# A hand-ordered cross-attention kernel: a new order of all engines and transfers up to the first attention sum of the end stage, banks picked one by one, and row-by-row exponentials in four words

## The chip, the cores and the metric

The kernel runs on one core of a Trainium2 chip, as one program. The metric is device time in microseconds, here the median of three runs. A profile is one execution of the same program, taken by the hardware profiler; its span is the time from the first to the last instruction.

## What is computed

Two batches of 2048 tokens (640 channels) attend with 20 heads of 32 channels to two sets of 77 keys: text, and image prompts with weights of their own. All data are float32.

```python
q = split_heads(x @ Wq.T)
k, v = split_heads(text @ Wk.T), split_heads(text @ Wv.T)
out_text = merge_heads(softmax(q @ k.T / sqrt(32)) @ v)
k_ip, v_ip = split_heads(ip @ Wk_ip.T), split_heads(ip @ Wv_ip.T)
out_ip = merge_heads(softmax(q @ k_ip.T / sqrt(32)) @ v_ip)
return (out_text + out_ip) @ Wo.T + bo + x
```

## The kernel before

All matrices come with the contracted dimension first. The channels lie in 5 chunks of 128, which are 4 heads (g = 0 to 3) each. Ten pairs q = (batch, chunk) are worked through, each as two units of 1024 tokens, u = 2q and 2q + 1. A unit has two halves h of 512 tokens, or 8 blocks of 128 tokens, and these go in three groups s of 3, 3 and 2 blocks. A group is 4 heads x n blocks x 2 key sets of 77, so 24 or 16 rows of 77 scores for each token.

PSUM has eight banks of 512 numbers (`banks`, named bank_67 to bank_74 in the program). A group of scores fills four, one for each head; before the change these are always the first or the last four (`halves`).

The order of the whole kernel is written out by hand, as a list of words (`SCHEDULE`). The loop at the end emits them one after the other; each engine does its own in that order, and waits only for data, or for a place that is still read. The words:

- q.u.h: queries of unit u and half h, five matmuls of 128 x 512 (L206); cq copies them out of their bank, scaled, on ScalarE (L220).
- k.c.y and v.c.y: keys and values of chunk c and key set y (L144); ck and cv copy them (ScalarE); SQ.c turns the values in squares of 32 (VectorE, L154); VS.q.half spreads them over the partitions with 8 small transfers (SP, L160).
- Rs.u: scores of group s (L242). Ks.u: their four copies, one a bank, to SBUF (ScalarE, L254). M: row maxima (VectorE, L290). S: subtraction (GpSimd, L304). E: exponential of the group (ScalarE, L310). D: row sums (VectorE, L315), I: their reciprocals (L320), N: the product with them (GpSimd, L325), T: a transposition in squares of 32 (VectorE, L332).
- A.q: attention sum of a pair (L341), which needs all six T of its two units and both spreads; CA copies it (L364, L368).
- o, p, m: products with Wo for the two batches (L480, L499, L509); co and cm add them to x and bo on VectorE; G and W are sums on GpSimd that these products use.
- LK, LQ, LX, LO load weights of keys and values, weights of queries, tokens, and Wo. SF and SS fetch a part of x to `acc` and store a result. All these are issued by SP, strictly in order.

Three sets name groups that go other ways. In BIASED the subtraction falls away: each row's exponential takes its maximum as a bias, with one instruction a row (`exponential_of`, L278). In DIRECT the maxima (L293) and these exponentials also read the scores from PSUM, so K falls away and the banks stay taken until the exponentials have read them. In SUMMED the exponential sums its row too (a second instruction a row), so D falls away.

From 19 us to 427 us TensorE goes through these words up to A.9, the attention sum of the last pair. Then 66 products of a fast matrix scheme (L887) end the kernel.

Of the kernel before, what the change touches and what calls it, by code (L numbers as in the profile page):

```python
# [9 lines left out]
F32 = mybir.dt.float32  # L10
# [10 lines left out]
def kernel(  # L21
# [25 lines left out]
    nc = tc.nc  # L47
# [3 lines left out]
    G = P // D  # L51
# [13 lines left out]
        (11, 0), (12, 0), (13, 0), (13, 2), (14, 0), (14, 2), (15, 1), (15, 2), (18, 1), (19, 2),  # L65
    }
    BIASED = {
        (2, 2), (3, 2), (4, 2), (6, 2), (8, 2), (9, 2), (11, 2), (12, 1), (16, 2), (17, 2), (18, 2),
    }
    SUMMED = {  # L70
        (4, 2), (11, 2), (12, 0), (13, 0), (13, 2), (14, 0), (15, 1), (15, 2), (16, 2), (17, 2), (18, 1),
        (18, 2), (19, 2),
# [13 lines left out]
    halves = banks[:G], banks[G:]  # L86
# [145 lines left out]
    def rows_of(u, s):  # L232
        return keys_of(u, s).rearrange("p n g (t l) -> p (n g) t l", l=L)
# [36 lines left out]
    def exponential_of(u, s, ps=None, den=None):  # L270

        n = GROUPS[s][1]
        for g in range(G):
            for t in range(n):
                for x in range(2):
                    row = rows_of(u, s)[:, t * G + g, x]
                    one = t * G + g, slice(x, x + 1)
                    nc.scalar.activation(  # L278
                        row,
                        row if ps is None else rows_in(ps[g], n)[:, t, x],  # L280
                        AF.Exp,
                        bias=maxs[(u, s)][:, *one],
                        accum_out=None if den is None else den[:, *one],
                    )
# [300 lines left out]
    for t in range(2):  # L585

        ps = halves[t][G - 2 + t]
        project_kv(t, ps)
        for b in range(B):
            nc.scalar.copy(kT[:, 0, b, t, :], keys_in(ps)[:, b])  # L590
# [73 lines left out]
    def emit(word):  # L664
        name, _, where = word.partition("@")
        k, *args = name.split(".")
        x, y = (*(int(a) for a in args if a.isdigit()), None, None)[:2]
        i = int(k[1:]) if k[1:].isdigit() else None
        if k[0] == "R":
            at[name] = halves[int(where)]  # L670
            scores(x, i, at[name])
        elif k == "A":
            at[name] = halves[int(where)]
# [262 lines left out]
```

## Time and profile before

| | |
|---|---|
| device time, median of 3 runs (lowest to highest) | 495.86 us (495.68 to 496.0) |
| the profiled execution: span | 494.6 us |
| transfers | 69.38 MB in 67105 packets, mean 140 GB/s |
| costliest line of TensorE, L206 | 34% of the chain that ended last |
| costliest line of GpSimd, L325 | 176.0 us in 60 instructions |
| costliest line of VectorE, L332 | 115.9 us in 60 instructions |
| costliest line of ScalarE, L254 | 85.3 us in 200 instructions |

A row of the chain or of a timeline gives start, length, engine, line, and how many instructions were merged. An engine's row gives busy time and mean duration, then its idle time before the group and what ended that. SPq is SP's issue of transfers: its length is issue time only, and the landing comes later. Each matmul in float32 shows twice, so a query word is x10 and a group of 12 score matmuls x24.

### The profile page before, as it was taken

What the parts mean: (1) busy time and instruction counts of PE and PEld (TensorE: products, weight loads), DVE (VectorE), ACT (ScalarE), POOL (GpSimd) and SP (SyncE); (2) the same over time, 40 slices, a digit from 0 to 9 for tenths busy, and PEclk for the clock granted to TensorE, in tenths of its full rate; (3) what the DMA queues carried; (4) which work ended last, traced back from release to release, by engine and by line L of the source; (5) the groups of instructions that cost most, each with busy time, mean ns of one, the idle gap of its engine ahead of it and who ended that gap; (6) DMA issues with size and microseconds to landing.
All of it is one profiled execution on the core that took longest, in us unless ns stands there. A gap on an engine that the chain in (4) does not pass through costs nothing.

```text
span 494.6 us, 10484 instructions
## 1 busy us (share of the span) xinstructions
PE 489.1 (99%) x4116; PEld 287.7 (58%) x4116; DVE 413.9 (84%) x416; ACT 309.5 (63%) x1002; POOL 370.5 (75%) x158
## 2 busy tenths in 40 slices
PE   9999999999999999999999999999999999999997
PEld 5666648558557556456566654754755675444443
DVE  0069989989899989979988896687789898999996
ACT  1275788977687778677899786587889862100000
POOL 0069988988988988879886758475689899798700
PEclk9999999999999999999999999999999999999999
DMA  8992046203241724895540666455550212320125
GB/s 278 350 288 80 17 124 181 67 1 95 62 150 44 247 65 146 270 345 178 161 172 27 215 195 223 134 172 183 184 169 19 90 42 85 129 85 2 42 85 212
DMA packets 67105, 69.38 MB, mean 140 GB/s; under 512 B 5488, under 2 KB 47088, under 8 KB 67056
## 3 DMA queue, kind: packets, MB, share of 16 engines
q1 hardware_dynamic: 66048, 67.54, 43.7%
q10 hardware_dynamic: 1008, 1.18, 0.7%
q8 instruction: 32, 0.52, 0.4%
q14 instruction: 17, 0.14, 0.1%
HBM read 54.94 MB, written 10.49 MB: 132 GB/s over the span
## 4 chain that ended last, share of the span: by engine, by line
PE 96%; DMA 3%; ACTq 0%; ACT 0%; DVE 0%; DVEq 0%; issue 0%
PE bank L206 34%; PE bank L887 12%; PE bank L341 11%; PE bank L242 11%; PE bank L499 10%; PE bank L144 9%; PE bank L480 7%; PE bank L509 3%; DMA aT<-in_L_xattn_Wk_ip_dram 2%; DMA x<-in_x_dram 1%; ACTq L538 0%; ACT pb L254 0%; ACTq L552 0%; DVE acc L830 0%; DVEq L931 0%
## 5 line engine op out<-in xcount | busy, mean ns | idle before, releaser
L325 POOL TENSOR_TENSOR pb<-pb,rden 128x1848 f32<-128x1848 f32 (+1 forms) x60 | 176.0, 2943 | 30.4 <-DVE rden L320 23.6
L304 POOL TENSOR_TENSOR pb<-pb,mx 128x1848 f32<-128x1848 f32 (+1 forms) x39 | 121.6, 3129 | 55.4 <-DVE mx L290 55.3
L206 PE MATMUL bank<-x,wq 128*128 128x512 f32 x280 | 125.4, 598 | 0.1
L332 DVE STREAM_TRANSPOSE pb<-pb 128x1920 f32<-128x1920 f32 (+1 forms) x60 | 115.9, 1938 | 9.1 <-POOL pb L325 8.9
L290 DVE TENSOR_REDUCE mx<-pb 128x24 f32<-128x1848 f32 (+1 forms) x50 | 91.6, 1844 | 32.1 <-ACT pb L254 31.9
L254 ACT COPY pb<-bank 128x462 f32<-128x462 f32 (+1 forms) x200 | 85.3, 542 | 29.3 <-PE bank L242 28.9
L315 DVE TENSOR_REDUCE den<-pb 128x24 f32<-128x1848 f32 (+1 forms) x47 | 88.9, 1895 | 15.6 <-ACT pb L310 12.8
L206 PEld LDWEIGHTS bank<-x,wq 128*128 128x128 f32 x280 | 51.7, 190 | 60.0 <-issue 58.8
L310 ACT ACTIVATE pb<-pb 128x1848 f32<-128x1848 f32 (+1 forms) x39 | 65.6, 1684 | 17.5 <-POOL pb L304 17.4
L278 ACT ACTIVATE pb<-bank,mx 128x77 f32<-128x77 f32 x208 | 60.4, 387 | 6.5 <-DVE mx L293 6.5
L278 ACT ACTIVATE pb<-pb,mx 128x77 f32<-128x77 f32 x184 | 54.1, 356 | 1.9 <-DVE mx L290 1.8
L341 PE MATMUL bank<-pb,v 32*32 32x512 f32 x1600 | 55.2, 597 | 0.0
L206 PE MATMUL bank<-x,aT 128*128 128x512 f32 x116 | 51.8, 596 | 0.0
L242 PEld LDWEIGHTS bank<-kT,qT 32*128 32x128 f32 x1024 | 36.1, 184 | 21.6 <-issue 13.3
L144 PE MATMUL bank<-wo_ct,aT 128*128 128x154 f32 x320 | 46.0, 297 | 0.7 <-DMA aT<-in_L_xattn_Wk_ip_dram 0.4
L144 PEld LDWEIGHTS bank<-wo_ct,aT 128*128 128x128 f32 x320 | 43.0, 188 | 4.7 <-issue 3.0
L242 PE MATMUL bank<-kT,qT 32*128 32x154 f32 x1024 | 45.1, 305 | 0.0
L278 ACT ACTIVATION_READ_ACCUMULATOR pb<-bank,mx 128x1 f32 x168 | 44.0, 266 | 0.0
L341 PEld LDWEIGHTS bank<-pb,v 32*32 32x32 f32 x1600 | 29.0, 103 | 22.7 <-issue 10.1
L480 PE MATMUL bank<-aT,wo_ct 128*128 128x512 f32 x80 | 36.3, 595 | 0.0
L206 PEld LDWEIGHTS bank<-x,aT 128*128 128x128 f32 x116 | 21.4, 190 | 23.7 <-issue 23.5
L220 ACT ACTIVATE qT<-bank 128x512 f32<-128x512 f32 x32 | 19.3, 631 | 23.4 <-PE bank L206 23.4
(83 smaller groups left out, 524.2 us busy)
## 6 DMA issues: line engine op xcount, KB each, us to landing
x<-in_x_dram SPq DMA_DIRECT2D x20, 1280.0 KB, 6.7
out_dram<-acc SPq DMA_DIRECT2D x19, 256.0 KB, 2.9
x<-in_x_dram SPq DMA_DIRECT2D x17, 256.0 KB, 5.9
acc<-in_x_dram SPq DMA_DIRECT2D x16, 256.0 KB, 4.4
out_dram<-x SPq DMA_DIRECT2D x15, 256.0 KB, 2.0
v<-vS SPq DMA_DIRECT2D x160, 20.0 KB, 2.7
aT<-in_L_xattn_Wk_dram SPq DMA_DIRECT2D x5, 512.0 KB, 6.0
aT<-in_L_xattn_Wk_ip_dram SPq DMA_DIRECT2D x5, 512.0 KB, 5.5
```

Source lines behind the costliest of these rows:

```text
L144: nc.tensor.matmul(keys_in(out), loaded[n][:, k, :], cT[:, k, :, t, :], start=(k == 0), stop=(k == NCC - 1))
L206: nc.tensor.matmul(pq, weight_of(q)[:, k, :], xs[place_of(u, h)][:, k, :], start=(k == 0), stop=(k == NC - 1), skip_group_check=loose,)
L242: nc.tensor.matmul(ps[g][:, ts(t, 2 * L)], qTs[(u, h)][g * D : (g + 1) * D, ts(st, P)], kT[g * D : (g + 1) * D, c, b].rearrange("p t l -> ...
L254: nc.scalar.copy(keys_of(u, s)[:, :, g], ps[g][:, : n * 2 * L].rearrange("p (n l) -> p n l", n=n))
L278: nc.scalar.activation(row, row if ps is None else rows_in(ps[g], n)[:, t, x], AF.Exp, bias=maxs[(u, s)][:, *one], accum_out=None if den i ...
L290: nc.vector.tensor_reduce(mx, rows_of(u, s), AX.X, ALU.max, negate=negate)
L304: nc.gpsimd.tensor_tensor(rows_of(u, s), rows_of(u, s), maxs[(u, s)].unsqueeze(3).to_broadcast([P, n, 2, L]), ALU.subtract)
L315: nc.vector.tensor_reduce(den_of(u, s), rows_of(u, s), AX.X, ALU.add)
L325: nc.gpsimd.tensor_tensor(rows_of(u, s), rows_of(u, s), rdens[(u, s)].unsqueeze(3).to_broadcast([P, n, 2, L]), ALU.mult)
L332: nc.vector.transpose(p, p)
L341: nc.tensor.matmul(pa[r][g * D : (g + 1) * D, :], v4s[q % 2][rows, g, k, :], zones[rows, :, g, k, :], start=(k == 0), stop=(k == NK - 1),)
L480: nc.tensor.matmul(ps, wo[:, k, ts(NC - 1, P)], rows_of_attention(b, k)[:, i], start=(k == 0), stop=(k == NC - 1),)
```

## The change

Four things change. The order of words up to m4.3 and A.9 is a new one, while the words themselves stay nearly all the same; behind A.9 the order is as before, and only the numbers of banks differ. A group of scores or an attention sum no longer takes a half of the banks: its word lists four banks, in the order in which the heads take them. The exponential of a group is now four words, Es.u.0 to Es.u.3, one a head, so that other work of ScalarE can go between them; for a group that is neither DIRECT nor BIASED the first word does it all, and the others do nothing. And the three sets are drawn anew: DIRECT shrinks from ten groups to five, BIASED grows from 11 to 15, SUMMED has 13 as before.

```diff
     DIRECT = {
-        (11, 0), (12, 0), (13, 0), (13, 2), (14, 0), (14, 2), (15, 1), (15, 2), (18, 1), (19, 2),
+        (11, 0), (13, 0), (15, 1), (18, 1), (19, 2),
     }
     BIASED = {
-        (2, 2), (3, 2), (4, 2), (6, 2), (8, 2), (9, 2), (11, 2), (12, 1), (16, 2), (17, 2), (18, 2),
+        (0, 2), (2, 2), (4, 2), (5, 2), (6, 2), (9, 2), (11, 2), (12, 0), (12, 1), (13, 2), (15, 2), (16, 2),
+        (17, 2), (18, 2), (19, 1),
     }
     SUMMED = {
-        (4, 2), (11, 2), (12, 0), (13, 0), (13, 2), (14, 0), (15, 1), (15, 2), (16, 2), (17, 2), (18, 1),
-        (18, 2), (19, 2),
+        (0, 2), (2, 2), (4, 2), (5, 2), (6, 2), (11, 2), (12, 1), (15, 1), (15, 2), (17, 2), (18, 1), (18, 2),
+        (19, 2),
     }
...
-    halves = banks[:G], banks[G:]
...
-    def exponential_of(u, s, ps=None, den=None):
+    def exponential_of(u, s, g, ps=None, den=None):
         n = GROUPS[s][1]
-        for g in range(G):
-            for t in range(n):
-                for x in range(2):
+        for t in range(n):
+            for x in range(2):
...
-        "q.0.1@5 R0.0@0 cq.0.1 R1.0@1 K0.0 SF.0.0 q.1.0@0 K1.0 M0.0 LK.4 LQ.5 LK.5 M1.0 S0.0 R2.0@1 v.0.0@1 K2.0 "
+        "q.0.1@2 R0.0@6457 cq.0.1 R1.0@0132 K0.0 M0.0 K1.0 q.1.0@6 R2.0@0132 v.0.0@7 S0.0 cq.1.0 v.0.1@6 M1.0 "
...
         if k[0] == "R":
-            at[name] = halves[int(where)]
+            at[name] = [banks[int(n)] for n in where]
             scores(x, i, at[name])
...
                 elif direct or biased:
-                    exponential_of(
-                        x, i, ps if direct else None, den_of(x, i) if (x, i) in SUMMED else None
-                    )
-                else:
+                    if (x, i) in SUMMED and (x, i) not in dens:
+                        den_of(x, i)
+                    exponential_of(x, i, int(args[1]), ps if direct else None, dens.get((x, i)))
+                elif args[1] == "0":
                     exponential(x, i)
```

Three places show how the instructions move. The first is TensorE behind A.4. Before, the last rows of A.4 are followed by q.12.1 and then by the scores R0.11, in the last four banks:

```order
507 L341 MATMUL bank_73<-pb,v_0_80 32x512 x4
508 L341 MATMUL bank_74<-pb,v_0_80 32x512 x4
509 L206 MATMUL bank_68<-x_84,wq_75 128x512 x5
510 L242 MATMUL bank_71<-kT,qT_0_1766 128x154
511 L242 MATMUL bank_72<-kT,qT_0_1766 128x154
512 L242 MATMUL bank_73<-kT,qT_0_1766 128x154
513 L242 MATMUL bank_74<-kT,qT_0_1766 128x154
```

Now R0.11 follows at once, in four banks from both halves:

```order
507 L340 MATMUL bank_73<-pb,v_0_80 32x512 x4
508 L340 MATMUL bank_67<-pb,v_0_80 32x512 x4
509 L242 MATMUL bank_71<-kT,qT_0_1743 128x154
510 L242 MATMUL bank_69<-kT,qT_0_1743 128x154
511 L242 MATMUL bank_70<-kT,qT_0_1743 128x154
512 L242 MATMUL bank_68<-kT,qT_0_1743 128x154
```

The query word q.12.1 has moved behind R0.11, so that scores follow the attention sum directly.

The second place is ScalarE at the same point: the copies of A.4 (L364, L363 after the change) and the direct group E0.11, which reads its four banks (`mx_0` are its maxima). Before:

```order
232 L364 COPY aT<-bank_74 128x16x32
233 L310 ACTIVATE pb<-pb 128x8x154
234 L220 ACTIVATE qT_1_1957<-bank_68 128x512
235 L310 ACTIVATE pb<-pb 128x12x154
236 L278 ACTIVATE pb<-bank_71,mx_0_1968 128x77 x6
237 L278 ACTIVATE pb<-bank_72,mx_0_1968 128x77 x6
238 L278 ACTIVATE pb<-bank_73,mx_0_1968 128x77 x6
239 L278 ACTIVATE pb<-bank_74,mx_0_1968 128x77 x6
```

Now:

```order
242 L363 COPY aT<-bank_67 128x16x32
243 L277 ACTIVATE pb<-bank_71,mx_0_1927 128x77 x6
244 L277 ACTIVATE pb<-bank_69,mx_0_1927 128x77 x6
245 L277 ACTIVATE pb<-bank_70,mx_0_1927 128x77 x6
246 L309 ACTIVATE pb<-pb 128x12x154
247 L277 ACTIVATE pb<-bank_68,mx_0_1927 128x77 x6
```

The group moved ahead of other exponentials and of cq.12.1, and the exponential of another group stands between its third and fourth word. The word R1.11 takes bank_71 and bank_69, and o.0 takes bank_70.

The third place is SP around 190 to 205 us of the profile: spreads (L160), tokens (L188), weights of queries (L194) and Wo (L166). Before:

```order
52 L160 DMA v_0_80<-vS_0_93 32x160 x8
53 L468 DMA res<-in_x_dram 128x512
54 L188 DMA x_83<-in_x_dram 128x5x512
55 L194 DMA wq_75<-in_L_xattn_Wq_dram 128x5x128
56 L160 DMA v_0_80<-vS_0_93 32x160 x8
57 L188 DMA x_84<-in_x_dram 128x5x512
58 L166 DMA wo_ct<-in_L_xattn_Wo_dram 128x5x640
```

Now:

```order
50 L160 DMA v_0_80<-vS_0_93 32x160 x8
51 L194 DMA wq_75<-in_L_xattn_Wq_dram 128x5x128
52 L188 DMA x_83<-in_x_dram 128x5x512
53 L160 DMA v_0_80<-vS_0_93 32x160 x8
54 L166 DMA wo_ct<-in_L_xattn_Wo_dram 128x5x640
55 L188 DMA x_84<-in_x_dram 128x5x512
56 L160 DMA v_1_81<-vS_95 32x160 x8
```

The load of x_83 (LX.12.0, for q.12.0) now stands behind the weights LQ.6, and the load of x_84 (LX.12.1, for q.12.1) behind that of Wo.

More of the change, by code (lines that the diff above doesn't have):

```diff
@@ L268, in den_of @@
         return dens[(u, s)]
-    def exponential_of(u, s, ps=None, den=None):
+    def exponential_of(u, s, g, ps=None, den=None):
         n = GROUPS[s][1]
-        for g in range(G):
-            for t in range(n):
-                for x in range(2):
[L276 to L283, printed above, removed]
-                    )
+        for t in range(n):
+            for x in range(2):
+                row = rows_of(u, s)[:, t * G + g, x]
+                one = t * G + g, slice(x, x + 1)
+                nc.scalar.activation(
+                    row,
+                    row if ps is None else rows_in(ps[g], n)[:, t, x],
+                    AF.Exp,
+                    bias=maxs[(u, s)][:, *one],
+                    accum_out=None if den is None else den[:, *one],
+                )
     def maxima(u, s, ps=None, negate=False):
@@ L585 @@
     for t in range(2):
-        ps = halves[t][G - 2 + t]
+        ps = banks[G * t + G - 2 + t]
         project_kv(t, ps)
@@ L669, in emit @@
         if k[0] == "R":
-            at[name] = halves[int(where)]
+            at[name] = [banks[int(n)] for n in where]
             scores(x, i, at[name])
         elif k == "A":
-            at[name] = halves[int(where)]
+            at[name] = [banks[int(n)] for n in where]
             attend(x, at[name])
@@ L701, in emit @@
                 elif direct or biased:
-                    exponential_of(
-                        x, i, ps if direct else None, den_of(x, i) if (x, i) in SUMMED else None
-                    )
-                else:
+                    if (x, i) in SUMMED and (x, i) not in dens:
+                        den_of(x, i)
+                    exponential_of(x, i, int(args[1]), ps if direct else None, dens.get((x, i)))
+                elif args[1] == "0":
                     exponential(x, i)
```

142 rows, old and new, of the table SCHEDULE are left out of this document.

## The prediction

> **What bounds the kernel now.** I read the page first: busy shares, granted clock, chain.
>
> ```profile
> span 494.6 us, 10484 instructions
> PE 489.1 (99%) x4116; PEld 287.7 (58%) x4116; DVE 413.9 (84%) x416; ACT 309.5 (63%) x1002; POOL 370.5 (75%) x158
> PEclk9999999999999999999999999999999999999999
> PE 96%; DMA 3%; ACTq 0%; ACT 0%; DVE 0%; DVEq 0%; issue 0%
> ```
>
> TensorE is busy for 489.1 of 494.6 us and makes up 96% of the chain that ended last; its clock is granted in full throughout. So the span is the sum of TensorE's own work plus its waits. Next, the list of waits, for TensorE alone:
>
> ```profile
> PE bank L573 <- DVE pb L571: 1.1, 1, 1.1
> PE bank L144 <- DMA aT<-in_L_xattn_Wk_ip_dram: 0.4, 1, 0.4
> PE bank L144 <- DMA wo_ct<-in_ctx_dram: 0.3, 1, 0.3
> ```
>
> All three lie before 19 us, in code that the change leaves as it is. What remains must be looked for inside the busy time, in the chain of waits in order of time (start, length, what):
>
> ```profile
> 19.37 4.29 PE bank L206 x10
> 25.45 4.49 PE bank L206 x10
> 29.94 0.74 PE bank L242 x16
> 91.96 1.74 PE bank L242 x38
> 116.65 1.52 PE bank L242 x40
> 129.06 1.74 PE bank L242 x38
> 166.16 1.75 PE bank L242 x40
> 203.34 1.03 PE bank L242 x24
> 204.38 0.53 ACT pb L254
> 228.53 1.67 PE bank L242 x39
> 230.23 1.10 PE bank L499 x4
> 273.35 1.76 PE bank L242 x40
> 287.55 1.06 PE bank L499 x4
> ```
>
> Two things are to be seen. First, a query word (L206 x10) takes 4.29 us after other full-array work and 4.49 us after scores: 0.20 us for leaving the small tiles. Scores (L242) take 0.74 and 1.52 us for 16 and 40 matmuls, so 0.0325 us each and 0.22 us once per stretch. Second, 40 scores (or 38 recorded of 40) take 1.74, 1.74, 1.75 and 1.76 us at 92, 129, 166 and 273 us in place of 1.52. At 203 us the stretch and its wait for a copy last 1.6 us in place of 1.52, and at 228 us 39 scores with the next product last 2.8 us in place of 2.58. These are short waits for a copy that must empty a bank, 0.1 to 0.24 us each: **about 1.3 us** in all. No wait in the stretch up to the last attention sum is for a DMA.
>
> The Trainium skill (Perfetto Trace Analysis, Identifying the Most-Contended Engine) says that matmul busy time is no good measure for TensorE, and that the busy share of weight loads is one. By that rule the 58% of the row PEld would leave room. The repeated rows above speak against room that an order could use; the rule is the last of the rivals.
>
> **The change, part by part.** The diff adds and removes no matmul. TensorE's words are the same 232, in another order. I counted by the two schedules up to A.9. Full-array words right behind scores or attention: 49 before (45 behind scores, 4 behind attention), 46 after (44 and 2). Stretches of scores: 46 before, 45 after. So 3 x 0.20 + 1 x 0.22 = **-0.8 us**. This is on the path, since nothing covers TensorE's own time.
>
> The other engines get about the same load. Five groups leave DIRECT and need a copy again (two of 12 blocks, three of 8: 2 x 4 x 0.59 + 3 x 4 x 0.44 = 10 us of ScalarE). Groups with exponentials row by row go from 21 to 20, so GpSimd has one subtraction more, 3.3 us. SUMMED stays at 13 groups, with two more small ones and two fewer large ones, which is under 2 us of VectorE. How much room they have, one row of busy times by stretch tells, from the start of A.1 to that of A.2; the row above it is the copy's:
>
> ```profile
> L254 ACT COPY pb<-bank 128x462 f32<-128x462 f32 x136 | 64.7, 590 | 16.6 <-PE bank L242 16.6
> ...
> core 0: us, PE busy (x) PEld busy (x) DVE busy (x) ACT busy (x) POOL busy (x), PEclk, DMA share, GB/s
> 105.72:142.82 37.10, 37.10 (x394) 23.73 (x393) 33.57 (x25) 26.35 (x60) 33.03 (x11) 1.00 0.37 102
> ```
>
> VectorE and GpSimd fill 90% of such a stretch. So 10 us more of ScalarE over ten stretches are covered by TensorE, and cost nothing as long as no copy comes late. What can cost is order: where a word of TensorE stands right behind the thing it needs. I walked the places of the new order where that distance is shortest, each from a fixed point of TensorE.
>
> *Copies.* K words now free banks one by one, and a group of scores takes a bank just freed as its last of four. R0.4, R0.8 and R0.10 still take a bank of a query word that ended only 16 scores (0.63 us) earlier; R0.6 no longer does. In before the three of this kind (R0.4, R0.6, R0.8) cost 0.22 us each; the bank now comes fourth, some 0.1 us later. The word o.1 stands behind a direct group as in before (0.24 us). I take 0.2 us for each: **+0.8 us**; bounds 0.3 and 0.9.
>
> *The direct group E0.11.* The rows of before:
>
> ```profile
> 221.94 2.20 DVE L293 TENSOR_REDUCE mx<-bank 128x6 f32<-128x462 f32 x4
> 222.62 5.27 ACT L278 ACTIVATE pb<-bank,mx 128x77 f32<-128x77 f32 x24
> ```
>
> From the end of A.4: R0.11 takes 1.0 us, its maxima 0.1 + 2.2, then three of its four parts 3 x 1.3 + 0.1; the third bank is free after 7.3 us. TensorE reaches o.0, which writes that bank, after R0.11, q.12.1 and R1.11, 1.0 + 4.49 + 1.0 = 6.5 us. **+0.75 us**, of which R1.11 takes the first 0.3. In before the 5.27 us lay beside o.0, in a bank of the other half. The bounds are 0, if TensorE is late here anyway, and 1.2, if the maxima start late.
>
> *Transfers around q.12.0 and q.12.1.* SP issues in order. The rows of before (the first is the landing time of the 20 loads of 1.28 MB at L188):
>
> ```profile
> DMA to landing us min/median/max: 6.1/6.7/13.6
> 119.50 4.95 SPq L160 DMA_DIRECT2D v<-vS  x8
> 189.48 5.98 SPq L160 DMA_DIRECT2D v<-vS  x8
> 196.18 0.38 SPq L188 DMA_DIRECT2D x<-in_x_dram  x1
> 197.17 7.21 SPq L160 DMA_DIRECT2D v<-vS  x8
> 204.48 0.53 SPq L188 DMA_DIRECT2D x<-in_x_dram  x1
> 205.05 0.52 SPq L166 DMA_DIRECT2D wo_ct<-in_L_xattn_Wo_dram  x1
> 205.68 0.47 SPq L188 DMA_DIRECT2D x<-in_x_dram  x1
> L254 ACT COPY pb<-bank 128x308 f32<-128x308 f32 x64 | 22.1, 440 | 12.7 <-PE bank L242 12.4
> L290 DVE TENSOR_REDUCE mx<-pb 128x16 f32<-128x1232 f32 x16 | 22.5, 1409 | 2.8 <-ACT pb L254 2.6
> ```
>
> In the new order SQ.4 stands behind M2.9, and VS.4.0 waits for SQ.4. From the start of R2.9: copies K2.9 begin after 0.8 us and take 1.4, M2.9 1.4, the first square 0.35, VS.4.0 4.95 to 5.98, LQ.6 0.55; then LX.12.0 lands 6.1 to 6.7 us after its issue. That is 15.6 to 17.2 us. TensorE reaches q.12.0 after R2.9, R1.9, three query words and R2.10 with R0.10, 16.1 us. So 0 to 1.1 us; I take **+0.2 us**, since SP is quiet before VS.4.0 and the 4.95 row is the nearest. Then LX.12.0 0.5, VS.4.1 5 to 7.2 behind these loads, the load of Wo 0.55 and only now LX.12.1, which in before went ahead of Wo. It is issued 15.5 to 18.7 us after R2.9 began. In before the load that took 13.6 us had one of 1.28 MB and Wo ahead of it; with Wo alone I put it between that and 6.7, at about 10. With VS.4.0 at 4.95 and VS.4.1 at 7.21 it lands at 27.7 us, and q.12.1 stands at 28.05. **0 us**; bounds 0 and 4.2 (18.7 + 13.6 - 28.05).
>
> *LK.14 behind VS.2.0.* The word v.3.0 stands 11 us earlier than in before, and its weights are loaded behind a spread.
>
> ```profile
> aT<-in_L_xattn_Wv_dram SPq DMA_DIRECT2D x5, 512.0 KB, 5.5
> ```
>
> From the start of v.2.1: the word and its copy last 2.8 us, M0.5 and I2.4 keep VectorE until about 3.3, then the first square 0.35, VS.2.0 4.95, and 5.5 us to landing: 14.1 us. TensorE gets to v.3.0 after v.2.1, three score words, three others and R2.6, 15.3 us. **0 us**; bounds 0 and 1.0 (a spread of 5.98).
>
> *Ends of chains before A.n.* VectorE's main rows:
>
> ```profile
> L332 DVE STREAM_TRANSPOSE pb<-pb 128x1920 f32<-128x1920 f32 x40 | 86.4, 2161 | 5.5 <-POOL pb L325 5.5
> L315 DVE TENSOR_REDUCE den<-pb 128x24 f32<-128x1848 f32 x35 | 72.0, 2058 | 11.7 <-ACT pb L310 10.5 <-ACT pb L278 1.0
> L290 DVE TENSOR_REDUCE mx<-pb 128x24 f32<-128x1848 f32 x34 | 69.5, 2049 | 29.4 <-ACT pb L254 29.3
> ```
>
> Behind K1.17 and up to A.8 VectorE has 21 words: five maxima and sums and three transposes of these kinds, and thirteen shorter ones, 26.5 us when the 0.08 us by which neighbours overlap is taken off. It starts them 3.75 us after R1.17 began: 30.3 us. TensorE takes 30.3. A.5 and A.6 come out as close. I take +0.1 us each for A.5, A.6 and A.8, **+0.3 us**; bounds 0 and 1.5. Before A.9 the group (19,1) now goes row by row:
>
> ```profile
> 254.75 6.10 ACT L278 ACTIVATE pb<-pb,mx 128x77 f32<-128x77 f32 x24
> ```
>
> From the end of A.8 E1.19 starts when K0.19 is done (6.7 us), takes 6.1, and a quarter of E2.19 1.3 (5.27 / 4): 14.1 us. p.0, which needs that bank, stands at 14.4. **0 us**; bounds 0 and 0.5. The Trainium skill (ScalarE: Activation LUTs, Rules for kernel authors) budgets about 0.3 us per ACTIVATE plus 0.83 ns per element, so 0.36 for a row of 77 and 8.7 for 24: by it p.0 would wait 2.4 us, and the sum would be 2.4 us higher. The measured row says 6.1.
>
> Sum: -0.8 for the switches, -1.3 for the old short waits, +0.8 +0.75 +0.2 +0.3 for the new: **-0.05, taken as -0.25 us** because a wait at one place shortens the next (q.12.0's and E0.11's lie 6 us apart). The profiled execution's span is 494.6 us; the median of the runs, 495.86, lies 1.26 us above it, which I leave. Forecast **495.6 us**.
>
> **Rivals.** A measurement of this kernel can tell about 0.2%, or 1.0 us, from no change: from 494.87 to 496.85 counts as the same.
>
> *The new waits don't come.* If each place has the half microsecond of slack that my rows leave uncertain, only some 0.4 us of waits remain: -0.8 - 1.3 + 0.4 = -1.7, so 494.2 us. For it: the list of waits of before shows none for VectorE or a DMA in this part. Against: E0.11's 0.75 us come from two plain rows. This is also the most that the change can bring, 0.4%: with no wait at all it is -2.1.
>
> *The load behind Wo is late.* If LX.12.1 needs the 13.6 us of the one load that ran behind Wo in before, q.12.1 waits 1.0 to 4.2 us; less the 0.75 that it takes off E0.11, and on top of -0.25, this gives 0 to +3.2, so about 497.4 us. It decides from a landing time of some 11 us on. For it: the only measured load behind Wo. Against: that one had 1.28 MB more ahead.
>
> *The change takes off as much as it adds* is the forecast itself.
>
> *TensorE has room after all.* If its words could follow each other closer, VectorE's 33.57 us would set a stretch of 37.1, and nine of them would save some 32 us: 464 us. The rows of TensorE repeat to 0.01 us whatever stands beside them, so I give it 1%. The Trainium skill's rule on the share of weight loads, above, would allow it.
>
> **How the numbers follow.** Forecast 0.47, waits gone 0.29, late load and like slips (slower) 0.23, TensorE's room 0.01. Faster by over 0.2%: 0.30; within: 0.47; slower: 0.23. The range runs from all new waits gone (494.2, less 0.3 for what the old ones may add up to beyond 1.3) to the upper part of the late load (495.6 + 2.2): 493.9 to 497.8.
>
> **What would show it.** In the changed profile: TensorE's first 19 us equal; query words still 4.29 or 4.49; stretches of 40 scores at 92 and 166 us still near 1.7; a wait of o.0 (L479 there) or R1.11 on ScalarE near 221 us; q.12.1 at or right behind its load. The forecast is wrong if a DMA heads TensorE's list of waits with over 1.5 us, or if VectorE ends a wait before A.5, A.6 or A.8 by over 1 us.

## The result: 503.94 us, 1.5% slower

| | before | after |
|---|---|---|
| device time, median (lowest to highest) | 495.86 us (495.68 to 496.13), 5 runs | 503.94 us (500.81 to 505.76), 5 runs |
| ratio, with its 95% interval | 1 | 1.0154 (1.0127 to 1.018) |
| span of the profiled execution | 494.6 us | 499.0 us |

The forecast was 495.6 us, with a range up to 497.8. The profiled execution of the changed kernel is its shortest run, 500.81 us. So two things are to be explained: 4.4 us that the profile shows, and up to 5 us more that the other runs have, while before its runs agreed within 0.5 us. One run among the experiments below took 2835.2 us, each matmul of 128 x 512 lasting 3.0 us at a granted clock given as 1.0; nothing in its profile says why.

The page of the changed kernel (busy times; granted clock in 40 slices; the queue by which instructions come; shares of the chain that ended last):

```profile
span 499.0 us, 10417 instructions
...
PE 489.8 (98%) x4116; PEld 289.1 (58%) x4116; DVE 417.6 (84%) x401; ACT 314.4 (63%) x991; POOL 371.8 (74%) x159
...
PEclk9999999999999999999999999999999999999999
...
q8 instruction: 32, 0.52, 0.5%
...
PE 71%; DVE 13%; ACT 7%; POOL 3%; DMA 3%; issue 2%; ACTq 0%; DVEq 0%; POOLq 0%
```

TensorE's own work is the same. The chain, which was TensorE's for 96%, now goes through VectorE and ScalarE. TensorE's waits (what for, us in total, times, longest):

```profile
PE bank L498 <- DVE acc L529: 2.4, 1, 2.4
PE bank L572 <- DVE pb L570: 1.1, 1, 1.1
PE bank L498 <- DVE acc L523: 0.8, 1, 0.8
PE bank L242 <- issue: 0.8, 1, 0.8
```

The 1.1 us at the start were there before. New are 2.4 and 0.8 us for VectorE, and 0.8 us in which TensorE waited for nothing that the profile shows. I set each word of TensorE against a timetable of the same order without waits. By it, the difference of the two spans is: start -0.8 us (the first loads landed earlier), switches -0.8, short waits up to A.6 2.2 in place of 1.3 us (+0.9), m1.2 1.3 us late, m3.3 0.9, m7.3 2.6, and 0.4 in the products behind A.9. This sums to 4.5, against 4.4 measured. The -0.8 of the start is chance: among profiles with the same code up to 19 us, the first word q.0.1 starts anywhere from 18.2 us (after_vbest2) to 19.1 us (after_loads).

**The two waits for VectorE.** VectorE of the changed kernel, 403 to 414 us (start, length, operation, out<-in, size). V words are sums of 128 x 128 blocks of Wo for the end stage, X words sums of attention rows; the last letter says whether VectorE (d) or GpSimd (p) makes them.

```profile
403.39 1.63 DVE L883 TENSOR_TENSOR pb<-wo_ct 128x128 f32<-128x128 f32 x1
404.94 0.86 DVE L523 SCALAR_TENSOR_TENSOR acc<-bank,bo_sb,acc 128x256 f32<-128x256 f32 x2
...
410.25 0.22 DVE L883 TENSOR_TENSOR pb<-pb,wo_ct 128x128 f32<-128x128 f32 x1
410.50 3.40 DVE L881 SCALAR_TENSOR_TENSOR pb<-pb,wo_ct 128x128 f32<-128x128 f32 x1
413.83 0.67 DVE L529 TENSOR_TENSOR acc<-acc,bank 128x512 f32<-128x512 f32 x1
```

GpSimd at the same time (in brackets its idle time before, and what ended that):

```profile
402.51 2.35 POOL L889 TENSOR_TENSOR aT<-aT 128x1024 f32<-128x1024 f32 x1
...
410.47 3.29 POOL L324 TENSOR_TENSOR pb<-pb,rden 128x1848 f32<-128x1848 f32 x1 [1.48 <-DVE pb L883]
```

The first row on VectorE is V.F.0.d, the fourth V.Q.0.d. The same words on VectorE before the change, and GpSimd beside them:

```profile
392.38 0.25 DVE L866 TENSOR_TENSOR pb<-wo_ct 128x128 f32<-128x128 f32 x1
...
408.70 0.42 DVE L864 SCALAR_TENSOR_TENSOR pb<-pb,wo_ct 128x128 f32<-128x128 f32 x1
```

```profile
391.65 0.46 POOL L866 TENSOR_TENSOR pb<-wo_ct 128x128 f32<-128x128 f32 x1 [0.17 <-PE bank L341]
392.87 2.25 POOL L325 TENSOR_TENSOR pb<-pb,rden 128x1232 f32<-128x1232 f32 x1 [0.76 <-DVE rden L320]
...
408.94 5.54 POOL L325 TENSOR_TENSOR pb<-pb,rden 128x1848 f32<-128x1848 f32 x2
```

There V.F.0.d fell into GpSimd's idle time from 392.11 to 392.87 us, and V.Q.0.d began 0.24 us ahead of GpSimd's N1.19.

V.F.0.d has gone from 0.25 to 1.63 us and V.Q.0.d from 0.42 to 3.40. Each ends within 0.2 us of the GpSimd operation beside it (402.51 + 2.35 = 404.86 and 405.02; 410.47 + 3.29 = 413.76 and 413.90). Behind V.F.0.d stands cm5.3, behind V.Q.0.d cm6.3, which empty the banks that m3.3 and m7.3 want. Other words of VectorE are not long beside GpSimd: the two halves of cm5.3 at 404.94 us, which lie beside a subtraction of GpSimd from 404.83 to 408.16, take 0.43 us each and read one operand from PSUM, and maxima and row sums have one operand.

**The wait for nothing.** TensorE of the changed kernel around 350 us:

```profile
349.57 0.79 PE L242 MATMUL bank<-kT,qT 32*128 32x154 f32 x13
351.11 0.79 PE L242 MATMUL bank<-kT,qT 32*128 32x154 f32 x11 [0.75 <-issue]
351.83 1.99 PE L498 MATMUL bank<-aT,wo_ct 128*128 128x256 f32 x8
```

This is R0.17, right behind A.7. It stops in its middle, after 13 of its 24 matmuls; the fourteenth starts 1.04 us after the thirteenth.

### The profile page after: what moved, and what is told of

Read it like the earlier page. It is cut to its first block, busy times and chain, and to the rows that moved or that the text cites. A ratio compares the mean times of both kernels' runs of the same rounds, so it can differ in the third digit from the quotient of the medians.

```text
span 499.0 us, 10417 instructions
## 1 busy us (share of the span) xinstructions
PE 489.8 (98%) x4116; PEld 289.1 (58%) x4116; DVE 417.6 (84%) x401; ACT 314.4 (63%) x991; POOL 371.8 (74%) x159
## 4 chain that ended last, share of the span: by engine, by line
PE 71%; DVE 13%; ACT 7%; POOL 3%; DMA 3%; issue 2%; ACTq 0%; DVEq 0%; POOLq 0%
PE bank L206 25%; PE bank L904 11%; PE bank L242 8%; PE bank L498 8%; PE bank L340 8%; PE bank L144 5%; PE bank L479 4%; DVE mx L289 4%; ACT pb L277 4%; DVE pb L331 3%; PE bank L508 2%; DVE den L314 2%; POOL pb L324 2%; DMA aT<-in_L_xattn_Wk_ip_dram 2%; ACT pb L254 1%
## 5 line engine op out<-in xcount | busy, mean ns | idle before, releaser
L303 POOL TENSOR_TENSOR pb<-pb,mx 128x1848 f32<-128x1848 f32 (+1 forms) x40 | 124.0, 3109 | 55.2 <-DVE mx L289 55.1
L289 DVE TENSOR_REDUCE mx<-pb 128x24 f32<-128x1848 f32 (+1 forms) x55 | 99.9, 1834 | 34.1 <-ACT pb L254 33.9
L331 DVE STREAM_TRANSPOSE pb<-pb 128x1920 f32<-128x1920 f32 (+1 forms) x60 | 114.2, 1926 | 3.8 <-POOL pb L324 3.7
L254 ACT COPY pb<-bank 128x462 f32<-128x462 f32 (+1 forms) x220 | 93.1, 537 | 21.7 <-PE bank L242 21.1
L314 DVE TENSOR_REDUCE den<-pb 128x24 f32<-128x1848 f32 (+1 forms) x47 | 89.9, 1917 | 17.3 <-ACT pb L309 16.0
L277 ACT ACTIVATE pb<-pb,mx 128x77 f32<-128x77 f32 x264 | 83.7, 389 | 2.6 <-DVE mx L289 2.6
L309 ACT ACTIVATE pb<-pb 128x1848 f32<-128x1848 f32 (+1 forms) x40 | 66.8, 1673 | 13.1 <-POOL pb L303 12.8
L277 ACT ACTIVATION_READ_ACCUMULATOR pb<-pb,mx 128x1 f32 x168 | 40.0, 239 | 0.0
L498 PE MATMUL bank<-aT,wo_ct 128*128 128x256 f32 x128 | 32.7, 388 | 2.4 <-DVE acc L529 2.4
```

Source lines behind the costliest of these rows:

```text
L254: nc.scalar.copy(keys_of(u, s)[:, :, g], ps[g][:, : n * 2 * L].rearrange("p (n l) -> p n l", n=n))
L277: nc.scalar.activation(row, row if ps is None else rows_in(ps[g], n)[:, t, x], AF.Exp, bias=maxs[(u, s)][:, *one], accum_out=None if den i ...
L289: nc.vector.tensor_reduce(mx, rows_of(u, s), AX.X, ALU.max, negate=negate)
L303: nc.gpsimd.tensor_tensor(rows_of(u, s), rows_of(u, s), maxs[(u, s)].unsqueeze(3).to_broadcast([P, n, 2, L]), ALU.subtract)
L314: nc.vector.tensor_reduce(den_of(u, s), rows_of(u, s), AX.X, ALU.add)
L331: nc.vector.transpose(p, p)
```

## The experiments

Twelve runs were made: the changed kernel once more, one other kernel twice (after_vbest and after_vbest2), and nine others once. All compute the whole result. Line numbers differ by a few where the list of words takes fewer lines.

| kernel | median (range), us | ratio to before (95%) |
|---|---|---|
| after_again | 503.46 (502.31 to 504.45) | 1.0152 (1.0133 to 1.017) |
| after_vf_late | 502.32 (500.15 to 504.21) | 1.0128 (1.0096 to 1.016) |
| after_v3_late | 499.42 (499.16 to 499.47) | 1.0071 (1.0055 to 1.0088) |
| before_vf_beside | 501.01 (500.0 to 501.97) | 1.0103 (1.0081 to 1.0125) |
| after_v3_phase | 497.34 (496.98 to 498.3) | 1.0032 (1.0019 to 1.0045) |
| after_v3_loads | 498.62 (498.33 to 498.97) | 1.0056 (1.0039 to 1.0072) |
| before_phase | 499.19 (497.94 to 499.7) | 1.0064 (1.0046 to 1.0082) |
| after_vbest | 498.19 (496.76 to 499.13, and one of 2835.2) | 1.0044 (1.0031 to 1.0057) |
| after_vbest2 | 496.55 (one run) | |
| after_loads | 498.13 (497.53 to 498.41) | 1.0043 (1.0029 to 1.0056) |
| after_all | 496.56 (496.01 to 496.81) | 1.0009 (1.0 to 1.0018) |
| after_all3 | 496.62 (496.26 to 496.94) | 1.0015 (1.0006 to 1.0024) |

### The changed kernel again, and why its runs differ

> The changed kernel itself, once more, to see what of its loss is the same in every run. Theory (VectorE's small sums V.F.0.d and V.Q.0.d are held by GpSimd's long operations, and TensorE waits 0.9 and 2.6 us behind them): both waits are there again, with V.F.0.d near 1.6 and V.Q.0.d near 3.4 us in place of 0.25 and 0.42, and the span is at least 498. Rival (the long rows were an accident of one execution): they are short here, and the waits lie elsewhere. Open: which stretch holds the 2 to 5 us by which the other timed runs exceeded the profiled one.

Both waits came again to 0.01 us (0.93 and 2.56 by the timetable), m1.2 was again 1.26 us late, and the span was 500.5. The 1.5 us more lie behind the long wait. Stretches of this kernel (length, busy time and count by engine, then granted clock, DMA share, GB/s):

```profile
414.00:416.00 2.00, 1.66 (x6) 1.46 (x7) 2.00 (x3) 0.00 (x0) 1.47 (x1) 0.83 0.00 0
416.00:418.00 2.00, 2.00 (x5) 1.21 (x5) 1.14 (x3) 0.00 (x0) 0.78 (x1) 0.50 0.00 0
418.00:420.00 2.00, 2.00 (x5) 0.78 (x4) 2.00 (x2) 0.00 (x0) 1.71 (x1) 0.82 0.46 143
```

Right behind the wait TensorE's clock is granted at half for about 3.4 us: 2 x (0.17 + 0.50 + 0.18) = 1.7 us lost, the same as the 1.8 us by which p.3 and m4.3 fall back. In the first profile the same wait of 2.4 us left the clock at 1.00. So a wait of this length lets the clock fall in some executions and not in others, and costs 1.7 us more where it does.

### Moving the small sums in the changed kernel

```diff
-... G4.3 m6.3 V.F.0.d X.B.p@2 E1.19.0 ...
+... G4.3 m6.3 X.B.p@2 E1.19.0 ...
-... cm4.3 V.I.0.p V.T.0.d SS.3.3 ...
+... cm4.3 V.I.0.p V.F.0.d V.T.0.d SS.3.3 ...
```

> The changed kernel with one VectorE word moved: V.F.0.d stands right ahead of V.T.0.d, behind all of VectorE's other work ahead of A.9. Theory in its strong form (V.F.0.d makes VectorE late, so that N1.19 starts on GpSimd just as V.Q.0.d is reached): both waits go, the span falls by 3.5 us to about 495.5. Weak form (each word is held by itself): only the 0.9 us before m3.3 go, V.Q.0.d stays near 3.4 us, span about 498. Rival (VectorE is late there for another reason): no change, span 499.

The weak form holds by the trace (the medians alone, 503.46 and 502.32, have intervals that overlap). The wait before m3.3 is gone, and m7.3 still comes 2.2 us late. V.Q.0.d on VectorE:

```profile
412.30 3.34 DVE L879 SCALAR_TENSOR_TENSOR pb<-pb,wo_ct 128x128 f32<-128x128 f32 x1
```

and on GpSimd:

```profile
412.21 3.28 POOL L324 TENSOR_TENSOR pb<-pb,rden 128x1848 f32<-128x1848 f32 x1
```

GpSimd took N1.19 0.09 us ahead of VectorE's V.Q.0.d. So it is decided by tenths of a microsecond which of the two comes first. The span was 502.4, far above the expected 498, because v.4.1 came 1.75 us late in this execution, where the first profile has 0.38, and because the clock was granted at half twice, once behind v.4.1 and once behind m7.3, at 1.7 us each. The halt before v.4.1 is the second subject below.

With V.P.1.d and V.Q.0.d also moved there:

> The changed kernel with V.F.0.d, V.P.1.d and V.Q.0.d all moved to right ahead of V.T.0.d. Theory, either form: TensorE's waits before m3.3 and m7.3 go, span about 495.5, unless V.T.0.d, X.A.d or A.9 come late instead. Rival (VectorE is late for another reason): 499.

Both waits are gone, the median falls by 4.0 us against after_again, and the four runs lie within 0.3 us. The span is 497.4, not 495.5: v.4.1 is 1.6 us late here too, and the three sums, now ahead of V.T.0.d, make F25.1 wait 1.1 us for VectorE.

### One word moved in the kernel before

```diff
-... G5.3 T1.18 SF.3.3 SF.3.2 V.P.0.p SF.3.1 V.F.0.d I2.18 ...
+... G5.3 T1.18 SF.3.3 SF.3.2 V.P.0.p SF.3.1 I2.18 ...
-... cm1.3 M0.19 R2.19@1 ...
+... cm1.3 M0.19 V.F.0.d R2.19@1 ...
```

> The kernel before, with one VectorE word moved to where the change has it: V.F.0.d behind M0.19, beside GpSimd's X.B.p. Theory, strong form: this one word costs the kernel before what it costs the changed one, V.F.0.d 1.4 us longer and then V.Q.0.d held by N1.19, 2.5 to 3.5 us in all, span 497 to 498. Weak form: V.F.0.d is held, and TensorE waits 0 to 1 us: span 494.6 to 495.6. Rival (accident or another cause): span 494.6, V.F.0.d at 0.25.

This one word costs the kernel before 5.1 us. TensorE's waits, then VectorE's two words:

```profile
PE bank L499 <- DVE acc L530: 2.4, 1, 2.4
PE bank L499 <- DVE acc L524: 1.1, 1, 1.1
```

```profile
402.75 1.77 DVE L866 TENSOR_TENSOR pb<-wo_ct 128x128 f32<-128x128 f32 x1
...
410.01 3.40 DVE L864 SCALAR_TENSOR_TENSOR pb<-pb,wo_ct 128x128 f32<-128x128 f32 x1
```

The strong form holds here, with a span of 498.2, just above its range: V.F.0.d makes VectorE late, GpSimd starts N1.19 first (at 409.97 us), and V.Q.0.d, which was not moved, takes 3.4 us as well. The four runs fall in two pairs: 500.0 and 500.12 us at a mean granted clock of 1.000, 501.9 and 501.97 at 0.996 and 0.997. The 1.9 us between the pairs are near the 1.7 us of one fall of the clock; the slower pair left no trace, so this goes by the mean clocks alone.

### The halt in the middle of scores

The halts stand at a fixed place of TensorE's program. Counting all instructions of TensorE in each trace (weight loads, matmuls, sequencer), the first one behind a halt of this kind is:

```
kernel          us       instruction   modulo 256
after           351.11   6593          193
after_again     350.89   6593          193
after_vf_late   184.91   3521          193
after_vf_late   354.29   6593          193
after_v3_late   184.73   3521          193
after_v3_late   352.18   6593          193
```

The queue q8 of the page moves 32 packets of 16 KB, one for each 256 of TensorE's some 8300 instructions. The trace has the time of each. The packet that belongs to instruction 6593 runs from 348.70 to 349.67 us in the changed kernel, and TensorE goes on 1.44 us after its end; for 3521 in after_v3_late it ends at 183.31, and TensorE goes on 1.42 us later. In the kernel before these two packets end at 347.29 and 181.33 us, before TensorE needs them. Where the DMA engines are quiet, a packet starts soon after TensorE has come to the border one block earlier (the first at instruction 203, where that border is 193; the fifth at 1219, where it is 1217). In attention sums and the scores behind them, 256 instructions last only some 5 us. And the DMA engines were full there. The stretch from A.3, and that from A.7, after:

```profile
177.32:183.67 6.35, 6.35 (x179) 3.64 (x178) 5.01 (x6) 4.19 (x5) 4.61 (x2) 1.00 0.88 311
344.12:350.40 6.28, 6.24 (x174) 3.39 (x174) 4.92 (x4) 5.09 (x19) 3.12 (x1) 1.00 1.03 381
```

and before:

```profile
177.82:183.90 6.08, 6.08 (x178) 3.46 (x181) 4.82 (x6) 4.75 (x7) 5.41 (x2) 1.00 0.12 37
344.74:350.20 5.46, 5.46 (x162) 2.84 (x161) 2.21 (x4) 4.97 (x30) 4.33 (x3) 1.00 0.31 95
```

The last three numbers are granted clock, DMA share and GB/s: the share is 0.88 and 1.03, where it was 0.12 and 0.31. The new order of transfers put three loads of 1.28 MB in a row over A.7 and others over A.3. Two experiments change one side of this each, and a third makes the halt in the kernel before.

```diff
-    for _ in range(5):
-        nc.tensor.matmul(banks[0][:, :P], warm, warm, start=True, stop=True)
+    for n in range(48):
+        rows = slice(n % G * D, (n % G + 1) * D)
+        nc.tensor.matmul(banks[n % G][:, :P], warm[rows], warm[rows], start=True, stop=True)
```

> after_v3_late, with the five warm-up products ahead of the first load replaced by 48 small ones (32 rows, 128 columns): TensorE's whole program then stands 172 instructions later. Nothing else moves. Theory (TensorE's instructions come by DMA in blocks of 256; both halts stand at the same place modulo 256, 193, and come because 256 instructions in the attention sum last only 5.1 and 5.8 us while the loads hold up the block): the borders move out of R0.9 and R0.17, to where 256 instructions last some 8 us, and both halts (1.6 us ahead of v.4.1, 1.3 us ahead of m1.2) go. The start may come up to 1 us later. Span 497.4 - 2.9 + (0 to 1) = 494.5 to 495.5. Rival (the halts are a wait of R0.9 and R0.17 themselves, for a bank or a copy that the profile does not show): both stay, at the same words, and the span is 497.4 to 498.4.

Both halts are gone, though the DMA share over the same two stretches is 0.87 and 1.02, as full as in the changed kernel (0.88 and 1.03): full DMA engines alone do not make a halt. TensorE behind A.3 and behind A.7; of the words and transfers none has moved:

```profile
184.08 1.07 PE L242 MATMUL bank<-kT,qT 32*128 32x154 f32 x24
185.35 2.90 PE L144 MATMUL bank<-wo_ct,aT 128*128 128x154 f32 x20 [0.20 <-ACT aT L367]
...
351.48 1.07 PE L242 MATMUL bank<-kT,qT 32*128 32x154 f32 x24
352.48 1.78 PE L498 MATMUL bank<-aT,wo_ct 128*128 128x256 f32 x7
```

v.4.1 is still 0.27 us late, as in after_again: this part is a wait for the copy CA.3 (in brackets), and it is in all figures for v.4.1 above. The median falls by 2.1 us against after_v3_late; the spans are 496.5 in the profiled run and 495.2 to 495.6 in the others, where 494.5 to 495.5 was expected. The start came 1.5 us later, and q.12.1 now waited 0.7 us for its load, the one that the prediction's slower rival named (LX.12.1 behind Wo); it took 11.5 us from issue to landing here. In the changed kernel itself it took 10.0 us, and q.12.1 did not wait.

```diff
-... G6.2 LX.18.1 q.18.1@4 LX.19.1 SF.2.2 D2.16 ...
+... G6.2 SF.2.2 LX.18.1 q.18.1@4 LX.19.1 D2.16 ...
```

> after_v3_late, with one transfer word moved: SF.2.2, which waits until about 348 us for a store, stands ahead of LX.18.1 and LX.19.1 in place of behind them, so that these two loads of 1.28 MB are not queued during A.7. Theory (a block of TensorE's instructions is held up by the loads): the halt ahead of m1.2 shrinks from 1.3 us to 0 to 0.6, that ahead of v.4.1 (its loads untouched) stays at 0.3 to 1.7. Span 496.1 to 496.8, unless q.18.1 now waits for its load. Rival (hidden bank wait): 1.3 us stay, 497.4.

As expected: m1.2 is 0.3 us late in place of 1.3, v.4.1 still 1.2. F25.1 waited 1.7 us in place of 1.1, which I did not follow up, so the span is 497.0.

For the kernel before, the warm-up gets 26 such small products in place of five full ones:

> The kernel before, with the five warm-up products replaced by 26 small ones, so that its whole TensorE program stands 84 instructions later. In the kernel before no border of 256 lies inside an attention sum under full load of the DMA engines; after this shift one lies at the end of A.4, whose DMA share is 1.04, 256 instructions and 4.3 us behind the one before. Theory of the blocks: a halt of 0.8 to 1.6 us at the end of A.4, which the kernel before does not have; none of more than 0.5 us at A.0 to A.3 and A.8, where the share is 0.02 to 0.45 and a block took 3.7 us. Span 495 to 497. Rival (hidden bank wait): no halt, span 494.6 plus or minus 0.5 for the start.

TensorE of this kernel at A.4 and at A.6 (L341):

```profile
209.68 5.50 PE L341 MATMUL bank<-pb,v 32*32 32x512 f32 x159
216.17 0.58 PE L341 MATMUL bank<-pb,v 32*32 32x512 f32 x1 [0.99 <-issue]
```

```profile
300.83 4.91 PE L341 MATMUL bank<-pb,v 32*32 32x512 f32 x135
307.25 1.12 PE L341 MATMUL bank<-pb,v 32*32 32x512 f32 x25 [1.51 <-issue]
```

The halt at A.4 came where it was expected, at its last matmul, instruction 4289 or 193 modulo 256. A.6 has one too, at instruction 5825, again 193; I had not named it (the DMA share there was 0.75), and with it the span is 497.4, above the expected 495 to 497. No hidden wait of a score word explains halts inside attention sums that the kernel before does not have.

### Putting it together

V.P.1 and V.F.0 are given to GpSimd (V.P.1.p V.F.0.p behind V.P.0.p), and V.Q.0.d stands behind M1.19:

> The changed kernel with the three small sums put where GpSimd does not stand in their way and VectorE's tail is not longer: V.P.1 and V.F.0 go to GpSimd itself, behind V.P.0, and V.Q.0.d behind M1.19, where GpSimd waits. Theory: no wait of 0.9 and 2.6 us before m3.3 and m7.3 and none of 1.1 us before F25.1 as in after_v3_late; the two halts on instructions (0.3 to 1.6 and 1.3 us) stay. Span 495.1 to 496.6, time 496.9 to 498.4. Rival (moving the words late was what helped, not GpSimd's idleness): V.Q.0.d is long here too, and the waits are back.

The profile of this kernel comes from one further run:

> after_vbest again, for a profile. V.Q.0.d, behind M1.19 beside no GpSimd operation: 0.4 to 0.6 us. No wait of VectorE's before m3.3 and m7.3. The halt ahead of m1.2 is there (1.3 us), that ahead of v.4.1 anywhere from 0.3 to 1.7; span 495.0 to 497.3. Rival (V.Q.0.d is long wherever it stands): 3 us, and the wait is back.

VectorE of after_vbest2, and GpSimd beside it:

```profile
398.14 0.47 DVE L879 SCALAR_TENSOR_TENSOR pb<-pb,wo_ct 128x128 f32<-128x128 f32 x1
```

```profile
396.22 2.25 POOL L324 TENSOR_TENSOR pb<-pb,rden 128x1232 f32<-128x1232 f32 x1
```

V.Q.0.d takes 0.47 us, m3.3, m7.3 and F25.1 wait no longer, and the 1.1 us before m1.2 are what is left. GpSimd does not quite wait there: its operation lasts until 398.47 us, and V.Q.0.d ends 0.14 us behind that, like the held sums above. It is short because only 0.33 us of that operation were left. The run is also faster than the six others of this kernel in the table, so what their median has more, 1.6 us, is in no trace; the halt before v.4.1, which this profile does not have, may be part of it.

Then the halts were to be taken out by the transfers. One of the three moves:

```diff
-... T2.7 VS.3.1 N1.7 T1.7 LX.11.1 LX.11.0 ...
+... T2.7 LX.11.1 VS.3.1 N1.7 T1.7 LX.11.0 ...
```

> after_vbest (the sums V.F.0, V.P.1 and V.Q.0 out of GpSimd's way), with its original warm-up and three transfers moved: SF.2.2 ahead of LX.18.1 as in after_v3_loads, LX.11.1 ahead of VS.3.1, so that fewer loads are queued when A.3 starts, and LX.12.1 ahead of the load of Wo. Theory (the blocks of TensorE's instructions are held up by queued loads): both halts go without the price at the start that the shifted warm-up has; m1.2 starts at most 0.3 us late and v.4.1 0.3 us; span 493.6 to 494.4, time 495.4 to 496.2, at or just under the kernel before. Rival (a load that is moved makes A.3, q.11.1 or q.18.1 wait instead, or the halt at A.3 comes from LX.10.1 alone, which is not moved): span 494.5 to 496.

A miss. With LX.11.1 ahead of it, VS.3.1 took 10.1 us to issue in place of 6.6, LX.11.0 went out 4.5 us later and lay over A.3 more than before; v.4.1 was 1.3 us late. m1.2 was 0.4 us late, near the expected 0.3, and F25.1 waited 0.7 us. And by the instruction count:

> The changed order with all three costs taken out at once: the sums V.F.0, V.P.1 and V.Q.0 as in after_vbest, 46 small warm-up products in place of five (164 instructions later, so that no border of 256 falls into an attention sum or the scores behind it), and LX.12.1 ahead of the load of Wo, as in the kernel before. Theory (these are all of the loss; the rest of the new order is worth what the short waits and the fewer switches add up to, about nothing): span 494.0 to 495.0, time 495.8 to 496.8, and runs that lie within 0.6 us of each other, since nothing makes TensorE wait long enough for its clock to fall. Rival (the new order loses somewhere else as well): span 495.5 or more.

The span of the profiled run is 495.0, the median time 496.56, 1.0009 (1.0 to 1.0018) of before, with eleven runs within 0.8 us. No halt is left, and no wait for VectorE but the one of 1.1 us at the very start, which all these kernels have. Its first rows show what it still loses, about 1 us at the start (its second query word starts at 19.53 us; in the changed kernel's first profile it is 18.45):

```profile
1.05 1.18 PE L574 MATMUL bank<-pb 32*32 32x32 f32 x92 [1.05 <-DVE pb L570]
3.75 3.78 PE L578 MATMUL bank<-x,aT 128*128 128x256 f32 x8 [1.51 <-DMA aT<-in_L_xattn_Wq_dram]
7.32 8.15 PE L206 MATMUL bank<-x,aT 128*128 128x512 f32 x16
```

> after_all with another warm-up: 44 small products and three of the old full ones behind them (168 instructions later than the changed kernel). In after_all the 92 small matmuls lasted only 1.18 us, TensorE then idled 1.51 us, and its first products ran slow (8.15 us for 16 of 128 x 512, in place of 7.03). Theory: with TensorE busy until the first load these are 7.03 again, the second query word of the first unit starts near 18.3 in place of 19.53, and the span is 493.4 to 494.2, time 495.1 to 496.0, at or just under the kernel before. Rival (the start is set by the loads): 494.5 to 495.0 as after_all.

The rival holds. With TensorE busy up to 3.8 us, its first load landed at 4.39 and the 16 matmuls took 7.37 us; the second query word started at 19.40. So no version that beats the kernel before was found, and why the first load landed later here is open.

## Why the prediction was wrong

It predicted 495.6 us, and named as steps:

- **Switches, -0.8 us.** Right: the timetable of the new order without waits ends 0.8 us earlier, and measured words fit it within 0.1 us between the waits.
- **Old short waits -1.3, new ones +2.05.** The sum was near, 2.2 in place of 1.3, but by luck. The term for the copies was right: R0.4, R0.8 and R0.10 cost 0.2 each, and o.1 0.4 where 0.2 was taken. The other 1.25 us of the new waits (E0.11, q.12.0's load, A.5, A.6 and A.8) did not come. Four waits that it had not named (before k.3.1, q.6.1, v.4.1 and q.13.0, 0.2 to 0.4 each) made up for them. The two marked rows of 40 scores came out as said, 1.80 us each, near 1.7:

```profile
91.17 1.80 PE L242 MATMUL bank<-kT,aT 32*128 32x154 f32 x40
```

- **E0.11, +0.75 us.** Wrong: R1.11 and o.0 follow each other without a wait.

```profile
221.30 1.07 PE L242 MATMUL bank<-kT,qT 32*128 32x154 f32 x24
222.30 4.13 PE L479 MATMUL bank<-aT,wo_ct 128*128 128x512 f32 x9
```

  I had let the exponentials begin behind all four maxima. They begin behind the first bank's, at 217.64 us, 1.5 us sooner. The two rows that the step was built on say so: there the maxima begin at 221.94 us and last 2.20, and the exponentials begin at 222.62.
- **Loads: q.12.0 +0.2, q.12.1 0, v.3.0 0.** None of the three waited for its load, and the load behind Wo took 10.0 us, the estimate of about 10. But this step priced a load only by its own landing. What a queue of loads does to the blocks of TensorE's own instructions has no place in the prediction: it cost 1.3 us before m1.2 and 0 to 1.5 us before v.4.1 (its lateness less the 0.27 us for CA.3).
- **"Ends of chains before A.n": +0.3, and before A.9 "0 us; bounds 0 and 0.5".** This is the step that failed. A.5, A.6 and A.8 did not wait. Before A.9 the walk followed ScalarE to p.0 (which came 0.1 us late; the row-by-row exponentials took 4.10 us for 16, 0.26 each, so the measured row was right there). The estimate of 0.36 us for a row from the Trainium skill (ScalarE: Activation LUTs, Rules for kernel authors) does not agree with these 0.26. The walk did not follow VectorE, where the same order moved V.F.0.d from 392 us, with GpSimd idle, to behind M0.19, beside X.B.p and in front of cm5.3. And it took VectorE's durations as fixed. What came in place of its 0 us are the 3.5 us for which m3.3 and m7.3 waited.
- **Both rivals on the faster side, and the late load behind Wo,** did not decide anything. The mechanism that made it slower was none of those named, and neither sign of being wrong appeared: no DMA heads TensorE's list of waits, and A.5, A.6 and A.8 did not wait.

The rows that would have told it were in the trace of before. Its VectorE sums of 128 x 1024 (least, median and greatest duration in ns):

```profile
L872 DVE TENSOR_TENSOR pb<-aT x5: 1218/1475/3369, 427.4 to 460.0; 128x1024 f32<-128x1024 f32 x5
```

One form with 1.2 to 3.4 us does not have a fixed duration. The 3.37 us are the first of two sums that begin at 430.06 us, beside this operation of GpSimd:

```profile
429.06 3.28 POOL L872 TENSOR_TENSOR pb<-aT 128x1024 f32<-128x1024 f32 x1 [1.26 <-ACT aT L368]
```

The sum begins 1.0 us behind the start of that operation and ends 1.1 us behind its end; the shortest of this size takes 1.22. The rule for it is also in the Trainium skill (SBUF — State Buffer, SBUF: two separate sides): an operation of VectorE with two SBUF inputs and one of GpSimd share a pair of ports, and whichever starts first has it for the whole instruction. The traces agree: V.F.0.d and V.Q.0.d end 0.14 to 0.16 us behind GpSimd's operation. That rule spoke against this change, and the prediction did not weigh it.

So the median's 8.1 us are made of these: 3.5 us of held sums; 1.3 us of the halt before m1.2; 0 to 1.5 us of that before v.4.1; 1.7 us each time that the clock falls behind one of these waits; and, from the steps that were predicted, next to nothing. The held sums and the halt before m1.2 are shown by taking each away alone; the halt before v.4.1 went only together with the other, when the instruction count moved. For the clock it is shown that it falls behind a wait, but not what decides in which execution.

How much of each the median run had is an estimate, since only the first of its five runs left a trace. A fall of 1.7 us in some 500 takes 0.0034 off the mean clock. The spans of 502.2, 502.4 and 504.0 us have mean clocks of 0.997, 0.996 and 0.993, which fits one, one and two falls. The run of 500.9 us has 1.000: its 1.9 us above the profiled one are not the clock, and the halt before v.4.1 may be most of them, which is not shown.

## What to carry to other kernels

Where one form of a VectorE operation has durations that differ by a factor, look at GpSimd beside it before pricing any move; a short sum with both operands in SBUF belongs where GpSimd waits, or on GpSimd. Price a load not only by its own consumer: where it fills the DMA engines during dense small matmuls, TensorE's instructions come late. And when TensorE never waits long, its clock is steady: a new wait of 1.2 to 2.4 us costs itself and, in some runs, 1.7 us more.

## What the runs showed of the hardware that I had not expected

- TensorE asks for a block of 256 instructions only about when it reaches the block before: in the 13 traces of ordinary length no packet begins more than 45 instructions ahead of that border. Under a DMA share of 1.03 TensorE came to that border at 345.33 us and could go on with the next block at 351.11, 5.8 us later. In the kernel before, at A.3 with a share of 0.12, it came there at 179.09 us, and the packet had ended at 181.33. The Trainium skill (Runtime: NRT & Kernel Launch, Instruction fetch mechanics) has the 256 and the queue of its own, and calls the cost of the crossing mostly hidden; here it was not, in eight of the profiled executions.
- The clock falls behind shorter waits than I would have thought. In after_vf_late the halt ahead of v.4.1 was enough; two stretches of it:

```profile
185.00:186.00 1.00, 1.00 (x9) 0.84 (x10) 0.97 (x3) 1.00 (x4) 0.59 (x2) 0.79 0.00 0
186.00:189.00 3.00, 3.00 (x14) 3.00 (x13) 3.00 (x2) 1.30 (x3) 3.00 (x1) 0.50 0.02 5
```
